# One line of a conv, feed-forward and LoRA kernel: seven more idle products at the start, and a new order for all 1,848 steps

## The chip, the core and the metric

The kernel runs on one core of a Trainium2 chip. The metric is the device time of one execution in microseconds (us). Five engines matter. TensorE does the matrix products (PE in the profile, its weight loads are PEld), VectorE is DVE, ScalarE is ACT, GpSimd is POOL and SyncE is SP. Each takes its instructions strictly from its own list, in the order in which the program recorded them. SP issues nearly all loads, ACT issues the stores and five small loads at the start.

## What is computed

```python
out = conv1d(x, weight, groups=4, kernel 9, padding 4) + (cond_128 @ c_weight.T)[:, :, None] + fside_S_0
# 64 samples, 64 channels, 1024 positions; the result, read as 8 blocks of 512 rows of 1024 numbers, is y
base  = y @ kernel + bias                               # 1024 x 1024 weights, all in float32
A_eff = gate x lora_A ;  B_eff = gate x lora_B          # 16 adapters of rank 32, mixed for each of 8 blocks
delta = (y @ A_eff.T) @ B_eff.T + (y @ lora_A_shared.T) @ lora_B_shared.T
return x + base + delta
```

## The kernel before

The rows are cut into 16 *pairs* p of 256 rows. A pair passes through four stages: its conv (four channel groups g), a transpose, the 1024 x 1024 product, and the addition of x, of the LoRA part and of the bias.

Every float32 operand of a product is split in two: ACT casts it to a high part (`hi_of`, line 265), and DVE or POOL subtracts that from the operand to get the low part (`lo_of`, line 270). Each product is then three: high by high, high by low, low by high. The last letter of a step says which engine subtracts, v for DVE, p for POOL and a for ACT.

The steps that the prediction speaks of:

- `warm` and `busy n` (lines 694 to 702): DVE fills a tile with ones, and TensorE multiplies it with itself n times, 256 columns each. Nothing reads the result.
- `twload`, `thi`, `tlo`, `twsum` load the conv's weights, split them, and add the two halves; `cwide` (line 727) widens the conditioning weights on DVE, `cmul` multiplies them on TensorE, `csum` (line 736) adds fside.
- `xload p g` (line 293) loads a group of a pair. For pairs 0 to 2 follow `xhi`, `xlo`, `conv` (six products of 512 columns, line 318), `evac` (line 374 on ACT, 376 on DVE). For the others `xdiff` (326), `xohi`/`xolo`, `xdhi`/`xdlo`, `convo` and `convd` (line 346; three and six products of 256 columns), `evmid` (364) and `evac` (378). `turned` (387) transposes.
- `wload k h` loads a piece of the weights in two DMAs, `fmm` and `fadd` (475, 479) add the shared LoRA to it, `whi` and `wlo` split it, `wsum` (485) makes the differences that the product scheme needs. 57 buffers hold pieces.
- Pair 0 takes the plain scheme, `plain p b k` (580, three products of 512 columns). From pair 1 on the scheme is one with seven products of blocks, `prod p j` (592, twelve products of 512 columns each), on sums of y made by `asum` on POOL (412) and split by `yhi` and `ylo`. Four of the seven open a new accumulator in PSUM; `mm` has five buffers.
- `lload`, `mix`, `mixout`, `mixput` (520, 528, 534, 542) mix the adapters and write them to DRAM; `aload` and `bload` (550, 556) read them back; `lora`, `axlow`, `axsum`, `axhi`, `axlo` and `delta` (602 to 660) apply them.
- `rload` (632) loads x once more, `keep` (636), `xsum`, `ysum`, `radd`, `yadd` (641 to 653) and `total` (666) add, `store` (669) writes 256 KB. `totalh` and `storeh` (675, 679) do the same with one half of the columns; half 0 is issued by SP, half 1 by ACT.

The order is written out: a string `ORDER` of 1,848 steps, which the kernel calls one after the other. What a step records is appended to the engines' lists, and the last loop of the function forbids anything else to reorder them:

```python
    steps = locals()
    for step in ORDER.replace("\n", " ").split(","):
        if step.strip():
            name, *args = step.split()
            steps[name](*(int(a) if a.isdigit() else a for a in args))
...
    for ins in list(nc.cur_bb.bb.instructions):
        if ins.engine in ORDERED:
            if ins.engine in last:
                tc.add_manual_dep(ins, last[ins.engine].name, nosync, reason="issue order")
            last[ins.engine] = ins
```

DMAs tell of their landing through eight semaphores, the *lanes*. The DMAs take them in turn, in the order of the steps, whether SP or ACT issues them, and a DMA that takes a lane again is issued only when the DMA eight places earlier has landed. So the order of the steps also decides which earlier DMA holds up a later one, and what stands behind it in the queue.

## Time and profile before

| | |
|---|---|
| median of three runs | 453.7 us (453.67 to 454.58) |
| the profiled execution, its own time | 454.4 us |
| its span, first to last instruction | 452.2 us |
| PE busy | 440.1 us, 97% of the span |
| DVE busy | 397.9 us, 88% |
| ACT, POOL busy | 248.2 us, 228.5 us |
| moved by DMA | 67.03 MB, 148 GB/s on average |
| granted TensorE clock over the span | 0.998 |

The profile is that of one execution. Its time is 2.2 us more than its span, and 0.7 us more than the median. In a timeline row the columns are the start, the duration, the engine, the line, the operation, out<-in and the shape; in brackets stand the idle time of the engine before the row and what ended it. A busy time of PE is a modelled one: the matmuls are pipelined, and a row of 0.39 us may follow the one before it by 0.23 us.

### The profile page before, as it was taken

The page shows a single profiled execution, that of the slowest core. Times are in us where ns is not written, and L with a number is a line of the kernel's source. Part 1 is how long each engine was busy: PE and PEld are TensorE (multiplying, and loading weights), DVE is VectorE, ACT ScalarE, POOL GpSimd, SP SyncE. Part 2 cuts the span into 40 slices and gives each one's busy share as a digit, 9 for nine tenths or more (in the row PEclk, how much of TensorE's full clock was granted, in tenths as well). Part 3 has the DMA queues.
Part 4 walks back from the last instruction along what each step waited for, and adds up shares of the span by engine and source line. Part 5 has one row for each costly group of instructions (what it writes and reads, how often), then busy time and mean ns, then how long its engine had stood idle before and what let it go on. Part 6 is the DMA issues. An engine that isn't in the chain of part 4 may idle for free.

```text
span 452.2 us, 7651 instructions
## 1 busy us (share of the span) xinstructions
PE 440.1 (97%) x2550; PEld 359.8 (80%) x2550; DVE 397.9 (88%) x619; ACT 248.2 (55%) x630; POOL 228.5 (51%) x201
## 2 busy tenths in 40 slices
PE   7999998999999999999999999999999999999996
PEld 6678655778888888888888887888888888888884
DVE  5899977999899989988899989979997998899792
ACT  3775385654564655546545555564575654644530
POOL 2675234556635574567565351543645364743563
PEclk9999999999999999999999999999999999999999
DMA  8899554366362364513356162444443534451533
GB/s 235 229 324 299 156 147 117 94 211 163 116 177 82 111 179 144 176 48 124 104 170 187 37 209 88 153 146 136 143 143 95 158 100 129 140 176 54 178 137 116
DMA packets 52486, 67.03 MB, mean 148 GB/s; under 512 B 6112, under 2 KB 34016, under 8 KB 52448
## 3 DMA queue, kind: packets, MB, share of 16 engines
q1 hardware_dynamic: 42512, 49.83, 38.8%
q10 hardware_dynamic: 9936, 16.73, 10.0%
q8 instruction: 20, 0.33, 0.3%
q14 instruction: 18, 0.15, 0.1%
HBM read 47.65 MB, written 18.87 MB: 147 GB/s over the span
## 4 chain that ended last, share of the span: by engine, by line
PE 78%; DVE 7%; issue 5%; DMA 4%; POOL 2%; ACT 1%; SPq 0%; ACTq 0%; POOLq 0%; DVEq 0%
PE mm_a L592 16%; PE mm_d L592 16%; PE mm_c L592 15%; PE mm_b L592 7%; PE cv L346 7%; PE cm L346 4%; PE axp L602 3%; PE cv L318 2%; PE mm_d L580 1%; PE mx L528 1%; DMA xt<-in_dram 1%; DVE y L270 1%; PE mm_a L580 1%; PE mm_c L580 1%; PE mm_b L580 1%
## 5 line engine op out<-in xcount | busy, mean ns | idle before, releaser
L592 PE MATMUL mm_a<-wh,y 128*128 128x512 f32 x240 | 79.6, 393 | 0.3 <-DVE y L270 0.3
L592 PE MATMUL mm_c<-wh,y 128*128 128x512 f32 x240 | 79.4, 391 | 0.2
L592 PE MATMUL mm_d<-wh,y 128*128 128x512 f32 x240 | 79.5, 392 | 0.0
L326 POOL TENSOR_TENSOR xf<-xt 128x256 f32<-128x256 f32 x52 | 38.0, 740 | 56.0 <-DVE xd L270 49.2
L364 ACT ACTIVATE md<-cm,cadd 128x64 f32<-128x64 f32 x208 | 48.0, 314 | 28.2 <-PE cm L346 24.7
L265 ACT CAST xd<-xf 128x512 fp32r<-128x512 f32 x52 | 32.6, 628 | 42.3 <-DVE xf L326 19.9
L592 PEld LDWEIGHTS mm_a<-wh,y 128*128 128x128 f32 x240 | 45.0, 188 | 11.1 <-ACT c L636 0.8
L265 ACT CAST y<-s 128x512 fp32r<-128x512 f32 x60 | 37.0, 624 | 29.8 <-POOL s L412 18.2
L592 PEld LDWEIGHTS mm_c<-wh,y 128*128 128x128 f32 x240 | 45.0, 188 | 10.0 <-ACT c L636 0.6
L592 PEld LDWEIGHTS mm_d<-wh,y 128*128 128x128 f32 x240 | 45.1, 188 | 9.7 <-issue 0.8
L387 DVE STREAM_TRANSPOSE z<-v 128x512 f32<-128x512 f32 x64 | 45.4, 709 | 1.9 <-ACT v L374 0.5
L592 PE MATMUL mm_c<-wl,y 128*128 128x512 f32 x120 | 46.9, 390 | 0.0
L592 PE MATMUL mm_a<-wl,y 128*128 128x512 f32 x120 | 46.9, 390 | 0.0
L592 PE MATMUL mm_d<-wl,y 128*128 128x512 f32 x120 | 46.8, 390 | 0.0
L270 DVE TENSOR_TENSOR y<-s,y 128x512 fp32r<-128x512 f32 x50 | 40.0, 804 | 6.5 <-ACT y L265 6.5
L346 PE MATMUL cv<-xd,th 128*128 128x256 f32 x208 | 45.4, 280 | 0.0
L378 DVE TENSOR_TENSOR v<-cv,md 128x512 f32<-128x512 f32 x52 | 35.7, 686 | 9.8 <-PE cv L346 4.2
L412 POOL TENSOR_TENSOR s<-s,z 128x512 f32<-128x512 f32 x15 | 22.0, 1465 | 37.3 <-DVE y L270 37.2
L270 POOL TENSOR_TENSOR xo<-xt,xo 128x256 fp32r<-128x256 f32 x25 | 21.7, 869 | 37.7 <-ACT xo L265 37.7
L592 PE MATMUL mm_b<-wh,y 128*128 128x512 f32 x120 | 39.8, 392 | 0.2 <-DVE r L666 0.2
L265 ACT CAST y<-z 128x512 fp32r<-128x512 f32 x49 | 30.5, 625 | 15.8 <-DVE z L387 4.1
L649 DVE TENSOR_TENSOR r<-r,c 128x512 f32<-128x512 f32 x41 | 35.9, 878 | 1.5 <-issue 1.1
(132 smaller groups left out, 1024.2 us busy)
## 6 DMA issues: line engine op xcount, KB each, us to landing
xt<-in_dram SPq DMA_DIRECT2D x64, 258.0 KB, 3.0
r<-in_dram SPq DMA_DIRECT2D x64, 256.0 KB, 3.6
out_dram<-r ACTq DMA_DIRECT2D x63, 256.0 KB, 2.8
ls<-in_dram SPq DMA_DIRECT2D x16, 256.0 KB, 4.3
br<-eff SPq DMA_DIRECT2D x48, 64.0 KB, 2.5
wr<-in_dram SPq DMA_DIRECT2D x16, 176.0 KB, 4.0
eff<-ls SPq DMA_DIRECT2D x16, 128.0 KB, 2.7
wr<-in_dram SPq DMA_DIRECT2D x16, 80.0 KB, 3.7
```

The source lines that it names most:

```text
L265: nc.scalar.copy(dst, src)
L270: engs[eng].tensor_tensor(dst, src, f32(hi), ALU.subtract)
L326: engs[eng].tensor_tensor(xdf[p, g][:, e], m, odd(p, g), ALU.subtract)
L346: nc.tensor.matmul(ps, a[:, w, g, :], b, start=(n == 0), stop=(n == 2))
L364: nc.scalar.activation(t[:, n], cpm[p, g][:, n], ACTF.Identity, bias=c[:, n:n + 1])
L378: nc.vector.tensor_tensor(v.rearrange("p n (i e) -> p e n i", e=2), cps.pop((p, g)), mid.pop((p, g)).unsqueeze(1).to_broadcast([P, 2, 4, H ...
L387: nc.vector.transpose(z[:, :, :, :, gg, :], vs.pop((p, g)).rearrange("p m j -> p (m j)"))
L412: engs[eng].tensor_tensor(t, m, n, op)
L580: nc.tensor.matmul(acc[p, BLOCKS[b]], m[:, kk, :], n, start=(k == 0 and q == 0), stop=(k == 7 and q == 2))
L592: nc.tensor.matmul(ps, a[:, k, :], b[bb, k], start=s, stop=(k == HK - 1 and q == 2), skip_group_check=not first)
L602: nc.tensor.matmul(axp[q * R:q * R + R, p % 2, :], a[:, k, :], zs[p, hf][:, k, :], start=k < 2, stop=k >= 6)
L649: engs[eng].tensor_tensor(r, r, cop[p, "x"], ALU.add)
```

## The change

All 1,848 steps are still there. No function is changed, and no line outside `ORDER`: `busy 22` has become `busy 29`, the steps stand in a new order, and 162 steps name another engine for their elementwise work. By kind, those on POOL go from 7 to 11 for `wlo`, 1 to 6 for `blo`, 4 to 9 for `radd`, 8 to 11 for `xdlo`, 0 to 1 for `sblo`, and from 52 to 45 for `xdiff`, 25 to 22 for `xolo`, 7 to 5 for `xlo`, 5 to 2 for `ysum`, 3 to 1 for `yadd`; `ylo` stays at 21, and the rest is on DVE. ACT gets two `evac` and one `mixout` more. The order was made anew by its planner, with the eight lanes in its account.

The beginning and the end of the string, before:

```
-small 1, twload 0, cwload, ctload, warm, gload, small 0, twload 1, thi 0, tlo 0 v, twsum, thi 2, tlo 2 p,
-busy 22, cwide, cmul, xload 0 0, xload 0 1, xhi 0 0, xlo 0 0 v, xhi 0 1, conv 0 0, xlo 0 1 v, xload 0 2,
-conv 0 1, csum, saload 0, gmask, saload 1, sahi 0, salo 0 v, evac 0 0 v, turned 0 0, sbload 1, xhi 0 2,
...
-yhi 0 0, xhi 1 1, fmm 0 1, fadd 0 1, xlo 1 1 p, fmm 2 0, ylo 0 0 p, wload 1 0, evac 0 3 a, fmm 1 0, fadd 1 0,
-whi 0 1, whi 0 0, turned 0 3, wload 1 1, whi 7 0, xload 1 3, wlo 7 0 p, conv 1 0, evac 1 0 a, fadd 1 1, wlo 0 1 v,
...
-delta 15 1, keep 15 3, delta 15 3, rload 15 3, rload 15 1, radd 15 1 p, prod 15 6, delta 15 0, rload 15 2,
-ysum 15 p, prod 15 4, radd 15 3 v, yadd 15 p, radd 15 2 p, total 15 3, delta 15 2, totalh 15 1 0,
-storeh 15 1 0, store 15 3, total 15 0, store 15 0, totalh 15 1 1, storeh 15 1 1, total 15 2, store 15 2
```

and after:

```
+small 1, warm, twload 1, busy 29, twload 0, cwload, gload, ctload, cwide, cmul, thi 2, small 0, thi 0, tlo 0 v,
+xload 0 0, xhi 0 0, tlo 2 p, xload 0 1, xlo 0 0 v, conv 0 0, twsum v, xhi 0 1, xlo 0 1 v, conv 0 1, sbload 1,
+sbhi 1, csum, evac 0 0 v, turned 0 0, xload 0 2, xhi 0 2, xload 0 3, saload 0, sblo 1 p, xlo 0 2 p,
...
+fadd 0 1, evac 0 3 a, fadd 1 0, conv 1 0, whi 7 0, fmm 4 0, turned 0 3, xload 1 2, xhi 1 2, wlo 7 0 v, fmm 3 0,
+wload 1 1, conv 1 1, fadd 1 1, wload 4 0, fmm 0 0, whi 0 1, wload 0 0, fadd 0 0, evac 1 0 a, plain 0 1 0,
+fadd 4 0, xlo 1 2 p, turned 1 0, whi 0 0, wlo 0 1 p, fmm 2 1, fmm 2 0, yhi 0 7, evac 1 1 a, conv 1 2, fmm 5 0,
...
+ysum 15 p, prod 15 1, yhi 15 6, axhi 15, axlo 15, delta 15 1, delta 15 3, prod 15 4, rload 15 3, delta 15 0,
+rload 15 1, radd 15 3 v, yadd 15 p, ylo 15 6 v, total 15 3, store 15 3, rload 15 2, radd 15 2 p, delta 15 2,
+total 15 2, store 15 2, radd 15 1 p, total 15 0, store 15 0, prod 15 6, totalh 15 1 0, totalh 15 1 1,
+storeh 15 1 1, storeh 15 1 0
```

(The lines are re-broken here; the steps are the string's own.)

## The prediction, made before the changed kernel ran

> **What bounds the kernel now.** I read the page first: its busy line and its chain.

> ```profile
> PE 440.1 (97%) x2550; PEld 359.8 (80%) x2550; DVE 397.9 (88%) x619; ACT 248.2 (55%) x630; POOL 228.5 (51%) x201
> PE 78%; DVE 7%; issue 5%; DMA 4%; POOL 2%; ACT 1%; SPq 0%; ACTq 0%; POOLq 0%; DVEq 0%
> ```

> TensorE is the bound. The change adds and removes no product that counts, so it can only gain the time in which TensorE waits or runs slowly: 452.2 - 440.1 = 12.1 us of idle span, and whatever hides in "busy". Next the waits, of TensorE alone (engine, line, engine and line waited for, us in total, times, longest):

> ```profile
> PE cv L318 <- ACT v L374: 1.9, 1, 1.9
> PE pc L733 <- DVE cwe L727: 1.7, 1, 1.7
> PE idle L701 <- DVE axt L695: 1.2, 1, 1.2
> PE mx L528 <- ACT ls L534: 0.7, 1, 0.7
> PE mm_d L580 <- POOL wl L270: 0.6, 1, 0.6
> PE cm L346 <- POOL xo L270: 0.6, 1, 0.6
> ...
> PE mm_a L592 <- DVE y L270: 0.3, 1, 0.3
> PE cm L346 <- DVE xo L270: 0.3, 1, 0.3
> ```

> They are single waits, spread out; none repeats with the pairs. The head holds 1.2 and 1.7, the rest of the run 4.6 (the six further rows above and one of 0.2). The remaining 4.1 us are the tail, after the last product. Then the timeline of the head, TensorE's rows:

> ```profile
> 1.18 5.06 PE L701 MATMUL idle<-axt 98*128 98x256 f32 x22 [1.18 <-DVE axt L695]
> ...
> 11.12 0.63 PE L318 MATMUL cv<-xsh,th 128*128 128x512 f32 x1
> 11.54 0.63 PE L318 MATMUL cv<-xsh,tl 128*128 128x512 f32 x1
> ...
> 14.17 0.40 PE L318 MATMUL cv<-xsh,th 128*128 128x512 f32 x1
> 14.41 0.39 PE L318 MATMUL cv<-xsh,tl 128*128 128x512 f32 x1
> ```

> The same product starts every 0.42 us at 11 and every 0.24 at 14: until 13.4 TensorE runs at about half its rate. The granted clock of these stretches is 1.00, so the spacing of the starts shows it and not the clock column. Nine conv products are slow, 9 x 0.19 = 1.7 us hidden in "busy". Last, the busy sums by stretch (length, then PE, PEld, DVE, ACT, POOL, clock, DMA share, GB/s):

> ```profile
> 20.00:30.00 10.00, 9.40 (x40) 7.26 (x39) 10.00 (x17) 7.85 (x18) 7.64 (x6) 1.00 0.92 272
> 30.00:40.00 10.00, 10.00 (x45) 7.99 (x43) 9.93 (x15) 6.33 (x16) 5.21 (x5) 1.00 1.01 308
> ```

> From 20 to 40 us DVE and the DMA engines are full as well. A TensorE that starts earlier is worth there only what they can follow. Later DVE has room: about 41 of 45 us.

> **The head, up to the last conv of pair 0's first two groups.** Seven more idle products of 0.213 us (22 take 4.7 start to start) keep TensorE at work from 1.18 to 1.18 + 29 x 0.213 = 7.4. Beside them: the conditioning weights land at 5.0 as before; `cwide` now stands first on DVE, 1.63 us in its row, to 6.6 (before 7.92); then tl 0.69 and xsl 0.77, to 8.1. ACT: table load to 4.42, two casts of 0.57, one DMA issue of 0.45 and xhi 0.62, to 6.7. POOL's tl, 1.79 from 5.0, to 6.8. So `cmul` runs without a wait from 7.4, eight products of 0.215 at the slow rate or half that, to 9.1 or 8.3, and conv begins there instead of at 9.69. The idle products cost nothing: what hides them is the arrival of the operands, until 6.6. If that cover went, they would cost 1.5.

> Whether conv then runs at the full rate: before, the 5.06 us of idle products were slow to the last, and the change came at 13.4, 3.8 us into the conv after a pause of 1.7. Now about 7 us without a pause stand ahead of it. I take full rate (7 us against 3.8). Head: 0.6 to 1.4 + 1.7 = **2.3 to 3.1 us**; xhi of groups 2 and 3, which wait for the buffers of conv 0 and 1, and the third load, no longer behind the second one's wait for a lane (1.8 us for bia in SP's waits), move with it.

> [...] The trace shows 4.7 us that were not enough. [...]

> **What DVE lets through of it.** I priced every step of both orders by its row (transpose 0.71, a 512-column subtraction 0.70 on DVE and 1.42 on POOL, xf 0.56 or 0.74, r and c 0.68 to 0.72, a product step 2.72, plain 0.70, conv 1.41) and compared how much TensorE work, idle products left out, stands ahead of equal DVE work. At 31.6 us of DVE work it is 28.7 before and 30.3 after; at 71.1, 79.3 and 90.1 the new order is ahead by 1.4, 2.0 and 1.9. Nothing is cheaper on DVE's own path: both orders start it near 5 us. So the head's 2.3 to 3.1 shrinks to 1.4 to 2.0 where DVE is full. I take **1.8**, from the stretch that decides; the ends are 0 and 3.0. Loads are no help and no harm: the weights stand at the same place (6.16 MB ahead of the fadd at 22.1 us of DVE work in both orders).

> Part of it is moved work: DVE's total falls by 4 us, ACT's grows by 3, POOL's by 8 (four wlo, five radd, five blo and three xdlo more, seven xdiff fewer). POOL is idle half the time, but not free of charge: DVE's subtractions with both inputs in SBUF take 0.68 alone and on average

> ```profile
> L270 DVE TENSOR_TENSOR y<-s,y 128x512 fp32r<-128x512 f32 x50 | 40.0, 804 | 6.5 <-ACT y L265 6.5
> L649 DVE TENSOR_TENSOR r<-r,c 128x512 f32<-128x512 f32 x41 | 35.9, 878 | 1.5 <-issue 1.1
> L378 DVE TENSOR_TENSOR v<-cv,md 128x512 f32<-128x512 f32 x52 | 35.7, 686 | 9.8 <-PE cv L346 4.2 <-ACT md L364 3.6 <-ACT y L265 0.7
> ```

> while v, which reads PSUM, stays at 0.69. Over all rows the excess is some 39 us for 228 us of POOL, 0.17 each; 8 us more cost DVE 1.4 of the 4 it is relieved of.

> **The middle.** Of the 4.6 us of waits the largest, 1.9, is conv 2 3 for an accumulator that an evac on ACT sets free. In the new order 6.1 us of products (plain 0 3 7, prod 1 1, prod 1 2) lie between conv 2 1 and conv 2 3, while ACT has 4.3 us queued ahead of that evac (two axlow, axhi, two whi, xhi, yhi), then 1.13, a transpose 0.71 and evac 0.69: 6.9. It is late by 0.8 instead of 1.9: 1.1 gained. From pair 2 on, chains from a product over the other engines to the next are longer than the products between them leave room for less often: twelve places with under 1 us to spare before, five after. New tight ones stand at the mixes: four leave 0.05 us, and the 0.7 row shows what a late one costs. I take **1.2**; ends -4 (next part) and +4.6.

> **The tail.** Before, the last total (0.69) and a full store follow the last product: 448.18, issue at 448.90, end at 452.2, 3.3 after the issue. Now `prod 15 6` is last, behind it two half totals of 0.42 and 0.41, and the second half's store, whose landing is 2.1 instead of 2.8: 0.10 + 0.83 + 0.03 + 2.6 = 3.6 against 4.1. **0.5**, between 0.3 and 1.0. `ylo 15 6` stands behind a radd that waits for a load and that for a store; it is due 9.9 us after delta 14 3, the product 11.8 after it.

> **The sum.** 1.8 + 1.2 + 0.5 = 3.5 us of the profiled 454.4: 450.9. The median shown is 0.7 lower: **450.2**.

> **Rivals.**
> - *Everything comes true* (0.12): full head 3.0, no waits left in the middle, tail 1.0: 8.6 us, 445.1. For it: the looser distances. Against: the two full engines at 20 to 40.
> - *The head is eaten* (0.13): TensorE starts earlier and waits for weights or DVE instead, and the middle trades old waits for new. Only the tail stays: 453.2, no difference. For it: 10.00 of 10 us on DVE. This is also the case in which the change doesn't do what it says.
> - *POOL holds TensorE up* (0.19), slower. Place: 20 to 50 us. Seven of the wlo ahead of pair 1's first product are on POOL, three before, and one of those three was waited for, 0.6. Four more at 0.6: 2.4. Ahead of `plain 0 0 0` POOL has xlo 1 2, wlo 0 1 and wlo 0 0, 4.1 us with 0.6 of whi, against 2.8 of products: 1.9. With DVE's 1.4 that is 5.7: 450.2 + 5.7 = 455.9. It decides from about 4 us of such waits on.
> - The forecast keeps 0.56.

> The range reaches from 445.4 to 456.0. A measurement of this kernel can tell 0.2%, 0.9 us, from no change: faster by more 0.68, within it 0.13, slower 0.19.

> **What would show it.** Conv products 0.24 us apart from the first one, beginning at 8.3 to 9.1; no wait of pc for cwe; at 40 us the lead over before is under 2.1. Wrong would be: conv still 0.42 apart; PE waits with POOL wl, xs or xsl as releaser of over 2 us together; waits of mx over 1 us; a tail of over 4 us.

## The result, and the profile after

The changed kernel takes 447.96 us (median of 4 runs, 447.25 to 450.92) against 453.99 of the kernel before: a ratio of 0.987, with a 95% interval of 0.983 to 0.991, so 6.0 us less where 3.5 were forecast. With the six executions of a second set (e5 below) the ten have a median of 449.1; by e5's own ratio it is 5.3 us less. The profiled execution took 447.5 us, one of the shortest of the ten, its span is 445.7 against 452.2. The page of the kernel after, its busy line and its chain:

```profile
PE 438.3 (98%) x2557; PEld 358.7 (80%) x2557; DVE 391.3 (88%) x615; ACT 251.2 (56%) x639; POOL 234.5 (53%) x202
PE 91%; DMA 4%; DVE 2%; issue 1%; SPq 0%; ACT 0%; ACTq 0%; DVEq 0%
```

TensorE's own work has grown from 78% to 91% of the chain that ends last; DVE fell from 7% to 2% of it. All of TensorE's waits in the kernel after (engine, line, engine and line waited for, us in total, times, longest):

```profile
PE idle L701 <- DVE axt L695: 1.2, 1, 1.2
PE cv L318 <- POOL xsl L270: 0.6, 1, 0.6
PE cv L346 <- DVE xd L270: 0.4, 1, 0.4
PE cv L318 <- DVE xsl L270: 0.4, 1, 0.4
PE mx L528 <- DMA ls<-in_dram: 0.4, 1, 0.4
PE cv L318 <- ACT v L374: 0.2, 1, 0.2
```

The waits of 1.9 (conv 2 3) and 1.7 (cmul) are gone, none on a `wl` of POOL has come, and all together they are 3.2 us, before 7.7. TensorE's timeline in the head:

```profile
1.18 5.38 PE L701 MATMUL idle<-axt 98*128 98x256 f32 x29 [1.18 <-DVE axt L695]
6.58 1.08 PE L733 MATMUL pc<-ctt,cwe 128*128 128x64 f32 x8
7.47 0.48 PE L318 MATMUL cv<-xsh,th 128*128 128x512 f32 x1
7.79 0.39 PE L318 MATMUL cv<-xsh,tl 128*128 128x512 f32 x1
8.02 0.39 PE L318 MATMUL cv<-xsl,th 128*128 128x512 f32 x1
...
11.62 0.51 PE L318 MATMUL cv<-xsl,th 128*128 128x512 f32 x1 [0.62 <-POOL xsl L270]
```

The 29 idle products take hardly longer than the 22 did: the spacing of their starts falls from 0.213 to 0.118 us after the eighteenth, at 5.0 us. `cmul` follows without a wait, and conv, 0.24 us apart, is at work from 7.47.

To say where the time went I use one measure for every run: the same TensorE work is priced by its usual spacing (0.227 to 0.235 us for 512 columns, half for 256, idle products left out), and the *lead* is how much earlier than in the trace of before a kernel stands at the same work. In us, with the time of before at the head of each column:

```
at (before's time)                     15.6  27.7  42.8  52.8  73.0  80.2  96.1 117.2 218.8 447.7
after                                   2.9   3.0   3.2   3.7   2.6   4.8   5.3   5.9   6.9   6.4
after, second trace (e5)                3.2   2.2   2.4   2.9   1.2   3.3   3.8   4.4   5.5   4.4
after, 22 idle products (e1)            2.9   2.0   2.2   2.7   0.1   2.2   2.7   3.3   4.4   3.5
after, no idle products (e11)           0.7   0.6   0.7   1.3  -1.2   0.9   1.4   2.0   3.1   1.9
before, 40 idle products (e2)           1.1   1.4   0.2   0.2   0.2   0.0  -0.7  -1.0  -1.1  -0.2
head of after, rest of before (e6)      2.9   2.7   2.6   2.6   2.6   2.6   2.7   2.1   2.0   2.1
head of before, rest of after (e7)     -0.4  -2.4  -2.3  -1.8  -3.6  -1.5  -1.0  -0.4   0.7  -0.1
before, one evac earlier (e4)          -0.1  -0.1  -0.8  -0.9  -0.8   1.3  -2.3  -2.6  -2.6  -2.6
after, two edits (e9)                   3.1   2.3   2.4   3.0   1.7   3.8   4.3   4.9   6.0   6.1
after, loads early (e12)                2.8   1.9   2.1   2.6   3.1   5.3   5.7   6.4   7.4   6.8
```

For the kernel after: 3.0 us from the head, 0.6 lost again between 43 and 73 us, some 2.1 gained at conv 2 3, the rest in small steps, and 0.1 in the tail. (The column at 52.8 hangs on the price of a `mix` product: there the kernel after has 20 of the first 32 behind it and the kernel before 2. At 43 neither has one, at 73 both have all.) Each row is one execution; the times given below are medians of 4 to 12. The traces of e2 and e7 are of long executions (454.8 against a median of 453.3, 454.0 against 452.0). In e1 to e4 the line numbers are five lower than in the profile of after (L313 is L318).

### The profile page after: what moved, and what is told of

Read it like the earlier page. It is cut to its first block, busy times and chain, and to the rows that moved or that the text cites. A ratio compares the mean times of both kernels' runs of the same rounds, so it can differ in the third digit from the quotient of the medians.

```text
span 445.7 us, 7717 instructions
## 1 busy us (share of the span) xinstructions
PE 438.3 (98%) x2557; PEld 358.7 (80%) x2557; DVE 391.3 (88%) x615; ACT 251.2 (56%) x639; POOL 234.5 (53%) x202
## 3 DMA queue, kind: packets, MB, share of 16 engines
q10 hardware_dynamic: 9936, 16.73, 10.2%
## 4 chain that ended last, share of the span: by engine, by line
PE 91%; DMA 4%; DVE 2%; issue 1%; SPq 0%; ACT 0%; ACTq 0%; DVEq 0%
PE mm_a L592 19%; PE mm_d L592 18%; PE mm_c L592 17%; PE mm_b L592 9%; PE cv L346 8%; PE cm L346 4%; PE axp L602 3%; PE cv L318 2%; DMA wr<-in_dram 2%; PE mx L528 2%; PE mm_a L580 1%; PE mm_c L580 1%; DMA ls<-in_dram 1%; DMA ctt<-in_dram 1%; PE mm_d L580 1%; PE mm_a L660 1%
## 5 line engine op out<-in xcount | busy, mean ns | idle before, releaser
L592 PE MATMUL mm_a<-wh,y 128*128 128x512 f32 x240 | 79.6, 392 | 0.0
L592 PE MATMUL mm_d<-wh,y 128*128 128x512 f32 x240 | 79.2, 391 | 0.0
L592 PE MATMUL mm_c<-wh,y 128*128 128x512 f32 x240 | 79.1, 391 | 0.0
L364 ACT ACTIVATE md<-cm,cadd 128x64 f32<-128x64 f32 x208 | 48.2, 315 | 44.8 <-PE cm L346 41.1
L326 POOL TENSOR_TENSOR xf<-xt 128x256 f32<-128x256 f32 x45 | 33.3, 747 | 49.4 <-DVE xd L270 39.4
L265 ACT CAST xd<-xf 128x512 fp32r<-128x512 f32 x52 | 32.5, 626 | 44.9 <-PE cv L346 20.7
L265 ACT CAST y<-s 128x512 fp32r<-128x512 f32 x60 | 37.2, 624 | 30.5 <-POOL s L412 15.3
L592 PEld LDWEIGHTS mm_a<-wh,y 128*128 128x128 f32 x240 | 45.1, 188 | 9.9 <-issue 0.4
L592 PEld LDWEIGHTS mm_d<-wh,y 128*128 128x128 f32 x240 | 45.1, 188 | 9.2 <-issue 0.2
L592 PEld LDWEIGHTS mm_c<-wh,y 128*128 128x128 f32 x240 | 45.1, 188 | 9.1 <-ACT c L636 0.2
L592 PE MATMUL mm_a<-wl,y 128*128 128x512 f32 x120 | 46.9, 391 | 0.0
L592 PE MATMUL mm_c<-wl,y 128*128 128x512 f32 x120 | 46.8, 390 | 0.0
L592 PE MATMUL mm_d<-wl,y 128*128 128x512 f32 x120 | 46.8, 390 | 0.0
L346 PE MATMUL cv<-xd,th 128*128 128x256 f32 x208 | 45.7, 282 | 0.4 <-DVE xd L270 0.4
L378 DVE TENSOR_TENSOR v<-cv,md 128x512 f32<-128x512 f32 x52 | 35.7, 686 | 7.7 <-PE cv L346 2.5
L270 DVE TENSOR_TENSOR xd<-xf,xd 128x512 fp32r<-128x512 f32 x41 | 34.5, 842 | 7.6 <-ACT xd L265 7.4
L270 DVE TENSOR_TENSOR y<-s,y 128x512 fp32r<-128x512 f32 x49 | 38.2, 782 | 3.0 <-ACT y L265 2.7
L592 PE MATMUL mm_b<-wh,y 128*128 128x512 f32 x120 | 39.6, 391 | 0.0
L346 PEld LDWEIGHTS cv<-xd,th 128*128 128x128 f32 x208 | 35.5, 188 | 2.4 <-DVE xd L270 0.6
L265 ACT CAST y<-z 128x512 fp32r<-128x512 f32 x49 | 30.6, 625 | 11.8 <-DVE c L641 4.5
L326 DVE TENSOR_TENSOR xf<-xt 128x256 f32<-128x256 f32 x59 | 33.7, 587 | 0.2
```

Of the source, the lines that this page charges most:

```text
L265: nc.scalar.copy(dst, src)
L270: engs[eng].tensor_tensor(dst, src, f32(hi), ALU.subtract)
L326: engs[eng].tensor_tensor(xdf[p, g][:, e], m, odd(p, g), ALU.subtract)
L346: nc.tensor.matmul(ps, a[:, w, g, :], b, start=(n == 0), stop=(n == 2))
L364: nc.scalar.activation(t[:, n], cpm[p, g][:, n], ACTF.Identity, bias=c[:, n:n + 1])
L378: nc.vector.tensor_tensor(v.rearrange("p n (i e) -> p e n i", e=2), cps.pop((p, g)), mid.pop((p, g)).unsqueeze(1).to_broadcast([P, 2, 4, H ...
```

## The experiments

**The idle products alone.** Four kernels change nothing but their number: the kernel after with 22 and with none, the kernel before with 40 and with 29.

```
e1:  ORDER of after,  busy 29 -> busy 22      e2:  ORDER of before, busy 22 -> busy 40
e11: ORDER of after,  busy 29 removed         e3:  ORDER of before, busy 22 -> busy 29
```

> The kernel after with 22 idle products in place of 29, nothing else changed. In the trace of the kernel after the spacing of the idle products falls from 213 to 117 ns after about 23 of them, 4.9 us from the first one. Theory A (the idle products bring the full rate): with 22 of them TensorE pauses from 5.9 to 6.6, before the rate has changed, and some 9 of the first conv products are 0.42 apart again, 9 x 0.19 = 1.7 us, plus up to 0.8 for eight slow products of cmul; of that 0.6 comes back, since the wait of conv 0 2 for a POOL subtraction falls away. So 1.1 to 2.0 us slower than after: 449.1 to 450.0. Rival B (DVE caps the head, as the forecast has it, so that of 3.0 us at most 1.8 are of use): under 0.6 slower, and TensorE's lead over the kernel before is the same 3.0 us at 25 us. Rival C (the order alone makes the head): no difference, and the conv products stand 0.24 apart.

> The kernel after without idle products. By the traces the full rate comes 3.8 to 7.2 us after TensorE begins to work without a pause, so with cmul beginning near 6.6 it comes at 10.4 to 13.8. Theory A (the idle products bring the rate forward): cmul 0.8 us longer, 5 to 13 conv products 0.42 us apart at 0.19 each, 1.0 to 2.5; less the wait of conv 0 2, which then falls away (0.4 to 0.6): 1.2 to 2.7 us slower than after, 449.8 to 451.5. Rival (the engines that feed conv decide, the rate of TensorE doesn't matter): under 0.6 slower.

> The kernel before with 40 idle products in place of 22, nothing else changed: at 213 ns for 23 of them and 117 ns for the rest they last to about 8.1 us, where the operands of cmul are there (7.97), so TensorE doesn't pause ahead of the conv. Theory A: conv begins at 8.7 to 9.1 in place of 9.69 and stands 0.24 apart from its first product; 2.3 to 2.6 us faster than before, and the same lead at 20, 40 and 75 us: 451.4 to 451.7. Rival B (DVE, full from 20 to 40 us in the order of before, caps the head): the conv is as fast, but the lead shrinks at 20 to 40 us to 1.0 or less: 453.0 or more. Rival C: no difference.

> The kernel before with 29 idle products, as many as the kernel after has: they end near 6.8, and TensorE then pauses for 1.2 us, since the order of before has the operands of cmul only at 7.97. If a pause of 1.2 us doesn't take the full rate away, it is like 40 products, 2.3 to 2.6 us faster than before. If it does, the conv is 0.42 apart for its first nine products and the time is that of before, 454.0.

Measured, as ratios to the kernel before with 95% intervals: e1 0.988 (0.986 to 0.991), e11 0.993 (0.991 to 0.995), e2 0.996 (0.995 to 0.998), e3 0.999 (0.996 to 1.001). The kernel after, in the same way (e5 below): 0.988 (0.985 to 0.992). The seven added products alone bring nothing that can be measured, in either order; the intervals leave room for some 2.0 us in the new one and 1.6 in the old. All 29 are worth 0.46% in the new order, 2.1 us by these ratios, give or take 2.0; against e1, with its 22, it is the same 2.1, give or take 1.5. TensorE's head in e3, and then in e11:

```profile
1.19 6.55 PE L696 MATMUL idle<-axt 98*128 98x256 f32 x29 [1.19 <-DVE axt L690]
8.01 1.97 PE L728 MATMUL pc<-ctt,cwe 128*128 128x64 f32 x8 [0.27 <-DVE cwe L722]
9.74 0.77 PE L313 MATMUL cv<-xsh,th 128*128 128x512 f32 x1
10.31 0.63 PE L313 MATMUL cv<-xsh,tl 128*128 128x512 f32 x1
10.74 0.63 PE L313 MATMUL cv<-xsl,th 128*128 128x512 f32 x1
```

```profile
6.61 1.94 PE L733 MATMUL pc<-ctt,cwe 128*128 128x64 f32 x8 [6.61 <-DMA ctt<-in_dram]
8.30 0.77 PE L318 MATMUL cv<-xsh,th 128*128 128x512 f32 x1
8.88 0.63 PE L318 MATMUL cv<-xsh,tl 128*128 128x512 f32 x1
```

In e3 all 29 are 0.213 us apart, TensorE stands still for `cwe` (0.27 us by the row above), and the conv products stay 0.43 us apart up to 15.0 us. In e1 the first conv product is already fast, though its 22 idle products were slow to the last: the rate had come by the end of a pause of 0.87 us (the idle time in the row of `cmul`, at 7.12). Its expected loss of 1.1 to 2.0 us did not show, so rival C can't be ruled out for the difference between 22 and 29; for none against 29 it fell. e11 came as theory A had it. (The expectations of e1 and e2 took the spacing to change after 23 products; in the trace of after it changes after 18, 3.8 us from the first.)

e2 was no clean test of a cap by DVE. In its trace the rate came only at 8.0 us, the 40 idle products lasted to 9.1, and conv began at 9.90, 0.2 later than before. By its median it is 1.6 us faster than before, as much as e6 below. In its trace the lead of 1.4 us at 28 us is 0.2 at 43, with DVE busy 39.0 of 40 us between 10 and 50 (before 37.9), which looks like rival B's cap. DVE's rows show something else: each stands 1.37 us earlier than in the kernel before, from 17 to 26 us of before's time, though DVE has no room there. Then a single subtraction takes 1.82 us in place of 0.68. DVE and POOL of the kernel before, then of e2:

```profile
26.90 0.68 DVE L270 TENSOR_TENSOR wl<-wr,wh 128x512 fp32r<-128x512 f32 x1
26.89 1.85 POOL L270 TENSOR_TENSOR wl<-wr,wh 128x512 fp32r<-128x512 f32 x1 [0.46 <-ACT wh L265]
```

```profile
25.54 1.82 DVE L265 TENSOR_TENSOR wl<-wr,wh 128x512 fp32r<-128x512 f32 x1
25.51 1.30 POOL L265 TENSOR_TENSOR wl<-wr,wh 128x512 fp32r<-128x512 f32 x1 [0.45 <-ACT wh L260]
```

POOL's row begins 0.010 us ahead of DVE's in the kernel before and 0.025 in e2, and it is POOL's that takes longer in the one and DVE's in the other (more of this in the last part). Of the lead 0.2 us are left behind this row; the later meetings, in both kernels, cancel. e3's trace loses 1.2 us at the same row.

**Head and rest.** e5 is the kernel after once more. e6 and e7 cut the two orders behind conv 0 3 and join them crosswise, each step once.

```
e6: ORDER of after up to "conv 0 3", then what is left of before's, in its order
e7: ORDER of before up to "conv 0 3", then what is left of after's, in its order
```

> The kernel after, unchanged, a second time and beside the next three. In six traces so far TensorE came to its full rate after 3.8 to 7.2 us of work without a pause, another value in each, so the head of the same kernel should differ from run to run. Theory A: with 29 idle products the full rate is there by 8.4 us at the latest, so at most 1.0 us of conv is slow; 447.3 to 449.0, and at no place behind the head a wait of over 1 us or a stretch at half rate. Rival (the first trace was a lucky one): 449 to 451, with waits of over 1 us for loads.

> The head of the new order, all steps up to conv 0 3 with their 29 idle products, and behind it the remaining steps in the order of before. Theory A (the old order of the rest can't use a head lead, since its DVE is full from 15 to 40 us, as the run with 40 idle products showed: lead 1.4 us at 20 us, 0.2 at 42): a lead of 2.4 to 3.0 at 15 us, under 1.2 at 45; the 2 us wait of conv 2 3 stays; 452.3 to 453.5. Rival B (the new head relieves DVE, which starts its subtractions and evictions earlier, and the lead lasts): over 2.2 us of lead at 45 us, 450.5 to 452.0.

> The head of before, all steps up to conv 0 3 with 22 idle products, and behind it the remaining steps in the new order. Theory A (behind the head the new order is worth 3.4 us by itself: 2.0 at conv 2 3, the rest in smaller waits, and no pause long enough to lose the full rate): no lead at 20 us, 2.0 to 4.0 from 80 us on; 450.0 to 452.0. Rival (it has that only with the head's lead, for its DVE and its loads then have slack): under 1.5 us faster than before.

Measured: e5 449.25 us, ratio 0.988 (0.985 to 0.992); e6 452.5, 0.996 (0.994 to 0.998); e7 451.95, 0.994 (0.992 to 0.996). So the new head is worth 1.9 us by itself, the new rest 2.8, and together they are the 5.3 to 6.0 of the whole within the intervals. In e6 the lead of 2.7 stays up to 96 us, behind the old order and its full DVE, as rival B had it; the median of 452.5 lies in theory A's range all the same, since the old order's later waits took 0.6 of the lead back. e7's profiled run was one of its longer ones (454.0): its lead falls to -3.6 at 73 us and rises by 4.3 up to 219, so it loses in the stretch where theory A saw no change and gains where it did. Why a full DVE lets the lead through is to be seen in its own head: in the kernel before it waits for TensorE three times there (0.77, 1.08 and 0.29 us). Its first eviction in before, in e6 and in e2:

```profile
12.64 0.69 DVE L376 TENSOR_TENSOR v<-cv,cadd 128x512 f32<-128x512 f32 x1 [1.08 <-PE cv L318]
```

```profile
9.79 0.69 DVE L376 TENSOR_TENSOR v<-cv,cadd 128x512 f32<-128x512 f32 x1 [0.76 <-PE cv L318]
```

```profile
11.75 0.69 DVE L371 TENSOR_TENSOR v<-cv,cadd 128x512 f32<-128x512 f32 x1
```

(In the kernel after it begins at 9.16.) In e6 each of DVE's rows is 2.6 to 2.7 us earlier than in before from 18 to 32 us; meetings with POOL take 0.9 of that, and before's own meetings give all but 0.1 back by 37. So e2 and e6 differ in how much earlier DVE starts and in which rows meet POOL, and no run shows a cap.

e5's median is 0.25 us above theory A's range and within the rival's, and its trace has one wait of over 1 us, which the first trace had not: 1.5, of conv 1 0 for a subtraction and not for a load. Its DVE rows, and then its POOL rows, at that place:

```profile
15.34 1.70 DVE L270 TENSOR_TENSOR xsl<-xt,xsh 128x516 fp32r<-128x516 f32 x1
```

```profile
15.20 1.28 POOL L270 TENSOR_TENSOR xs<-xt,xs 128x516 fp32r<-128x516 f32 x1 [2.12 <-ACT xs L265]
```

In the first trace DVE began that subtraction 0.2 us ahead of POOL's, and it took 0.70. Here it began 0.14 us behind it and took 1.70. The profiled run of e7 shows something else, behind a pause of 0.73 us. Its busy sums (length, PE, PEld, DVE, ACT, POOL, clock, DMA share, GB/s):

```profile
17.00:20.60 3.60, 2.52 (x9) 1.25 (x8) 3.54 (x3) 2.08 (x5) 3.19 (x3) 1.00 0.65 193
20.70:23.80 3.10, 3.06 (x8) 2.37 (x9) 3.00 (x6) 2.39 (x7) 1.28 (x2) 0.55 0.74 201
```

After a stretch in which TensorE was at work for 2.52 of 3.60 us, the granted clock is 0.55 for 3 us: eight products 0.42 us apart.

**One wait alone.** e4 takes the largest wait out of the kernel before, and changes nothing else.

```
-wlo 4 1 p, mixput 1 1, axlow 1, axsum 1, turned 2 0, whi 4 0, ... axhi 1, evac 2 1 a, ... keep 1 2, turned 2 1, axlo 0
+wlo 4 1 p, mixput 1 1, turned 2 0, evac 2 1 a, turned 2 1, axlow 1, axsum 1, whi 4 0, ... axhi 1, ... keep 1 2, axlo 0
```

> The kernel before with three steps moved: turned 2 0, evac 2 1 and turned 2 1 stand ahead of axlow 1 in place of behind axlow 0 and axhi 1, so that ACT doesn't do the small steps of the low-rank part ahead of the evac that frees conv 2 3's accumulator. Theory A (waits of TensorE add up one by one): the 1.9 us wait of conv 2 3 falls away or under 0.3, and with the 2.0 us that the lead of the kernel after grows by at that place the time falls by 1.6 to 2.0: 452.0 to 452.4. Rival (the wait is only passed on, to prod 1 2 or delta 0 0 1, whose small steps are now later on ACT): under 0.5 faster, and a new wait for ACT or DVE of over 1 us within 10 us behind it.

Measured: 456.25 us, 1.003 (1.001 to 1.005), slower. The rival was right, and too mild. The wait of conv 2 3 is gone and the lead rises by 2.1; then the evac's 1.15 us on ACT push the copies of two accumulators back, the second one's end from 80.6 to 81.7, while TensorE now needs its buffer at 79.1 and not at 80.4. The wait of e4 that is new, and the busy sums around it:

```profile
PE mm_c L587 <- ACT c L631: 2.5, 1, 2.5
```

```profile
78.00:81.50 3.50, 1.26 (x6) 0.68 (x4) 2.58 (x7) 3.32 (x9) 2.68 (x2) 1.00 0.38 108
81.70:84.80 3.10, 3.06 (x8) 2.41 (x9) 3.03 (x4) 2.57 (x5) 1.27 (x1) 0.54 0.00 0
```

Behind the longer pause the clock is 0.54 for 3 us, another 1.6 us. The wait of 1.9 hid a second limit close behind it, and a pause cost more than its length. The kernel before, e2, e3 and e6 all have the conv 2 3 pause; the half rate followed it in e2 alone (1.2 us).

**The engines.** e8 gives the 162 steps their old engines in the new order, e10 the new ones in the old order.

```
e8:  ORDER of after,  such as: xlo 1 0 v -> p, wlo 0 1 p -> v, evac 1 1 a -> v, xdiff 3 0 0 v -> p
e10: ORDER of before, the same letters the other way round
```

> The new order, with the engine letters of before on all of its 162 steps that had another one: DVE does some 4 us more by its rows, POOL 8 less, ACT 3 less. Theory A (the order, not the engines, makes the time): within 1.0 us of after, since DVE has 54 us of room over the run and POOL's price to DVE, 0.17 us each, gives some 1.4 of the 4 back. Rival (the letters are the relief without which DVE can't keep up from 15 to 40 us): 2 to 4 us slower than after, the loss at 15 to 50 us, with TensorE's waits for DVE there.

> The order of before with the engine letters of after: the same 162 letters as in the run of after with the old ones, which lost 34 us. Theory A (an order and its letters belong together: a subtraction in the queue of another engine waits there behind steps that it has nothing to do with): 15 to 40 us slower than before. Rival (the new letters are the better ones wherever they stand, since DVE has 4 us less to do): no slower than before, 452 to 455.

Measured: e8 489.6 us, 1.076 (1.072 to 1.079); e10 502.3, 1.106 (1.104 to 1.109). Both theories of e8 were far too low, and e10's loss of 48 us is above the range of the theory that it bears out. The same letters lose 34 us one way and 48 the other, so they are not better or worse by themselves. Waits of e8, from all engines:

```profile
POOL xf L326 <- DVE xd L270: 56.7, 23, 6.9
POOL xo L270 <- ACT xo L265: 37.1, 14, 5.4
ACT md L364 <- PE cm L346: 35.5, 22, 4.3
ACT y L265 <- POOL s L412: 32.0, 18, 7.1
```

POOL's `xdiff` alone stands 23 times behind a DVE step, and ACT behind POOL, while DVE's and POOL's busy shares, 86% and 47%, are no higher than before. Part of the loss is TensorE's rate: the traces record 10.2 us at half rate behind pauses in e8 and 23.9 in e10, which cost up to half of that. How much of the rest is queueing and how much the slowing of DVE beside POOL was not separated.

**A version that takes out what is left.** e9 makes two edits to the kernel after, e12 mends the second.

```
-xhi 1 1, xlo 1 1 p, xlo 1 0 v, turned 0 2, yhi 0 0             (e9 and e12)
+xhi 1 1, xlo 1 0 v, turned 0 2, xlo 1 1 v, yhi 0 0
e9:  lload 1 7, lload 1 3 moved ahead of rload 0 1; lload 1 2 ahead of aload 0
e12: lload 1 7, lload 1 3, lload 1 2 moved ahead of mixput 0 0
```

> The kernel after with two edits at the waits that its further traces show. In two of three traces conv 1 0 waits 1.5 us for a subtraction of DVE that takes 1.70 us in place of 0.70, beside a subtraction of POOL (xlo 1 1): here xlo 1 1 is done on DVE, behind turned 0 2. And the mixes of the second factor wait 0.4 to 2.0 us for loads that stand on SP behind the mixput of the first: three lloads are issued ahead of the loads of r and A. Theory A (each is a wait of TensorE by itself, and what follows has slack): 0.8 to 2.0 us faster than after, 446.8 to 448.0; no wait of conv for xsl or of mx for a load over 0.4 us. Rival (DVE, with 0.7 us more to do at its fullest stretch, passes the wait on, as with the evac moved in before): no difference, and a new wait for DVE between 20 and 40 us.

> As e9, but the three loads of the second factor (lload 1 7, 1 3, 1 2) are issued where SP sat idle in e9, for 8.3 us ahead of the first mixput (38.3 to 46.6), and not ahead of the loads of r and A; nothing stands between the mixputs and A's load that wasn't there in the kernel after. Theory A: neither a mix waits for a load nor lora for A (1.8 us in e9); about 1 us faster than e9's 447.8: 446.3 to 447.3. Rival (the early loads wait on SP for their buffers, which products free late, and hold the mixputs and A's load up): lora or the mixes wait 1.5 us or more, 447.8 or slower.

Measured: e9 447.82 us (447.20 to 447.99), ratio 0.986 (0.984 to 0.988); e12 447.09 (446.48 to 448.23), 0.986 (0.983 to 0.988). e9's second edit passed the wait on, from the mixes to the loads behind them:

```profile
PE axp L602 <- DMA ar<-eff: 1.8, 1, 1.8
```

In e12 SP issues the three loads while it has nothing else to do. All of TensorE's waits in e12:

```profile
PE idle L701 <- DVE axt L695: 1.2, 1, 1.2
PE cv L318 <- DVE xsl L270: 0.5, 1, 0.5
PE cv L346 <- DVE xd L270: 0.4, 1, 0.4
PE cv L318 <- ACT v L374: 0.2, 1, 0.2
```

Neither a mix nor lora waits, and the table shows it: a gain of 1.0 between 43 and 73 us where the kernel after loses 0.6 (1.2 in e5). The first edit holds too: conv 1 0 waits 0.5 us in e9 and e12, a little over the 0.4 of theory A, where e1 and e5 had 1.4 and 1.5. So the traces show the mechanism; the times do not resolve it, for e9 and e12 have the same ratio. e12's median is the lowest of all, 7.2 us below that of the kernel before beside it (6.5 by the ratio), but its interval overlaps that of the kernel after. The ten executions of e9 and e12 span 446.5 to 448.2, the ten of the kernel after 447.3 to 452.8.

## Why the prediction was right, and where it was wrong

- **The bound** was right: time came only from TensorE's pauses and slow stretches, and its idle span fell from 12.1 to 7.4 us.
- **The head** was right in size at TensorE: 3.0 us in the first trace, of the 2.3 to 3.1 forecast. That the idle products cost nothing there is shown by e11: without them `cmul` begins at 6.61, with them at 6.58. Where the rate comes later they can cost: in e6's trace `cmul` follows them at 7.27, and its last operand had landed at 6.6. Conv began at 7.47 and not at 8.3, since 11 of the 29 ran at 0.12 us and not at 0.213.
- **What brings the head** was right in kind, the full rate ahead of the conv, but not in the part of the seven products. In the new order, with `cwide` first on DVE, TensorE's pause ahead of `cmul` is short, and 22 did as well as 29 (e1); in the old order 29 brought no gain that can be measured (e3) and 40 brought 1.6 us (e2). The order alone, without idle products, has a lead of 0.7 us at 15.6 us (e11), with them it is 2.8 to 3.2. The forecast's "7 us against 3.8" was misread as well: before, TensorE worked without a pause from `cmul` on, at 7.97, so 5.2 us and not 3.8 went before the change, and in the after trace 3.8 were enough. When the rate comes was another time in each trace, 3.6 to 6.9 us after the first product where no pause came between, as the last part shows.
- **The step that failed** is "Nothing is cheaper on DVE's own path: both orders start it near 5 us. So the head's 2.3 to 3.1 shrinks to 1.4 to 2.0". The first half is true and does not carry the second: DVE starts at the same time but then waited 2.1 us for the slow TensorE, so the head freed it as well, and a DVE without room passes an earlier start on. The lead at 40 us, forecast under 2.1, was 3.2 (2.4 in e5), and e6 carries 2.7 through the old order. What does eat a lead there is a row of DVE that meets a running one of POOL: 1.5 us at conv 1 0 in e5, 1.2 in e2.
- **POOL's price** of 0.17 us of DVE per us was an average over the meetings of rows that the last part lists. DVE's total fell by 6.6 us where 4 less 1.4 was forecast; ACT grew by 3.0, POOL by 6.0 where 8 was forecast.
- **The middle** was mis-sized, 1.2 against 3.4 in the first trace and 2.2 in e5. At conv 2 3 the forecast gave 1.1 and left a wait of 0.8; 2.1 came, and no wait is left (TensorE is busy 10.00 of the 10 us from 70 to 80). The mixes were named as tight, and the stretch around them gave 0.6 back (1.2 in e5), but by loads behind the mixputs on SP (0.4 us of waits in the first trace, 1.2 in e5: over the 1 us that was to speak against the forecast) and not by their distances. What the sum lacked altogether is the rate that is lost behind a pause. The steps from 96 to 219 us, another 1.6, were not taken apart.
- **The tail** gained 0.1 and not 0.5. The last product ends at 441.67 and the two half totals by 442.5, as said, but from the last issue at 442.59 to the end of the span it is 3.1 us, not 2.6: half a store ends hardly sooner than a whole one, 3.3.
- **The sums.** 3.5 came as 6.0, or 5.3 by the second set: the DVE term and the middle were both too small. Two small sums do not close: 1.2, 1.7, 4.6 and 4.1 us make 11.6 of the 12.1 of idle span, and the range's lower end of 445.4 lies above the 445.1 of the prediction's own best case.
- **The rivals.** POOL does not hold TensorE up by itself: of 0.6 us of waits for it none is for a `wl`. By way of DVE it did in e5, 1.5 us at conv 1 0. Of the head nothing was eaten in the first trace, and 1.0 us in e5, at that place (3.2 to 2.2).

## What to carry to other kernels

A full engine is no cap on another one's head start while the first still waits for the second (here DVE for TensorE: 0.77, 1.08 and 0.29 us in the kernel before): look for its idle time in the head before pricing it. A pause of TensorE can cost more than its length (in e4 a wait of 2.5 us, and another 1.6 us at a clock of 0.54 behind it); expect behind each wait that is taken away the next one (e4, e9). One trace of a schedule as tight as this shows one draw: the same kernel waited 1.5 us at conv 1 0 (e5) or 0.4 (the first trace), by which of two rows began first. A change of engine is priced by what then stands in front of and behind the step in that queue, not by its duration: the same 162 letters cost 34 and 48 us where the order was not made for them.

## What the runs showed of the hardware

**How it is lost.** The half rate followed a pause of 0.73 us in e7 (TensorE busy 2.52 of the 3.60 us around it), one of 1.9 in e2 and one of 2.5 in e4, for 3.41 us each, and did not follow the same 1.9 in before, e3 and e6. The busy sums of e2, and then of before, at the same pause, in stretches of 3.41 us counted from the first change of the rate:

```profile
76.29:79.70 3.41, 1.53 (x7) 0.95 (x6) 2.47 (x5) 3.29 (x11) 3.02 (x3) 1.00 0.16 51
79.70:83.11 3.41, 3.41 (x9) 2.48 (x8) 3.28 (x6) 3.39 (x7) 0.93 (x1) 0.50 0.27 77
```

```profile
74.63:78.04 3.41, 2.37 (x11) 1.63 (x9) 2.26 (x6) 2.29 (x7) 3.41 (x3) 1.00 0.24 58
78.04:81.46 3.42, 2.47 (x9) 1.72 (x10) 2.83 (x6) 3.37 (x10) 1.46 (x2) 1.00 0.27 60
```

In e2 the pause lies in one stretch, with TensorE busy 1.53 of 3.41 us; in before an edge divides it, with 2.37 and 2.47 on the two sides (2.2 to 2.6 in e3 and e6). The 3.41 us ahead of the loss have 2.19 in e7 and 0.93 in e4. No limit comes out of these modelled sums: stretches with 1.61 in e8 and 1.71 in e10 kept the rate. The granted clock shows the slow stretches behind a pause (0.50 in e2 from 79.70 to 83.11), while the profile's column reads 1.00 for the first, slow one of every run: the record has no entry there, and only the spacing of the starts tells.

**DVE beside POOL.** A DVE subtraction of 512 columns with both inputs in SBUF takes 0.68 us alone (over 80 rows of the kernel after). Where a POOL instruction was running when it started, it ended 0.549 us after that one ended: in all 31 rows of the kernel after with over 0.2 us left, between 0.545 and 0.554, and the rows took up to 1.8 us. Where POOL started second, DVE kept its 0.68 (28 rows), and POOL's row was the longer one: its sums of line 412 took 1.29 undisturbed and 1.69 (median of 22) when they started during such a subtraction. Which of the two started first was worth 1.0 us at conv 1 0: DVE's row took 0.70 in the first trace and 1.70 in e5. Close starts went either way: with POOL 0.025 us ahead DVE's row was the long one in e2 (1.82), with POOL 0.010 ahead POOL's was in before (1.85, DVE 0.68).
